# Pools of their own for k and v, weight buffers in the place of k, and four chunks of the first feed-forward product ahead of the second

## The chip, the cores and the metric

The kernel runs on one core of a Trainium2 chip. The time is the device time of one execution in microseconds (us); the median of three runs is 2384.47 us. TensorE (PE) multiplies, VectorE (DVE) and ScalarE (ACT) do the elementwise work, GpSimd (POOL) and SyncE (SP) here mostly start transfers (DMA). Each of them works off its own queue in order: an instruction that waits holds all that stand behind it.

## The reference

Two layers, each with a normalisation ahead of it and a residual around it, over x of 2 x 2048 x 1024 in float32 (4096 tokens, width C = 1024):

```python
x = x + attn(layernorm(x), Wqkv, bqkv, Wo, bo)       # one head of width D = 256
x = x + ffn(layernorm(x), gate_w, up_w, down_w, fc1_w, fc2_w, expert_w, ln_gamma, ln_beta)

def ffn(h):
    w = sum(top_2(h @ gate_w))                        # of 8 experts, per token
    shared = relu(h @ up_w) ** 2 @ down_w             # 1024 -> 2048 -> 1024
    routed = ((h @ fc1_w) @ expert_w * w) @ fc2_w     # 1024 -> 512 -> 512 -> 1024
    return layernorm(shared + routed) * ln_gamma + ln_beta
```

## The kernel before, in words

Every product is made of three matmuls: each operand is split into a high part (a cast to fp32r, by ACT) and a low part (the rest, a subtraction, by DVE), and high x high, low x high and high x low are added up in one PSUM bank (`Pass3`, L117). All matmuls of this kind have line L130; tile names tell them apart: ps scores, po values, pw projection behind attention, pu first feed-forward product, pd second one.

The tokens are worked in eight blocks of 512 (NBLK = 8); blocks 0 to 3 are the first batch, 4 to 7 the second.

1. Q, K and V of all blocks (`qkv_block`, L408). k and v of a block are "units", tiles of 8 KB in each partition. Those of blocks 4 to 7 go to DRAM and are read back when the second batch begins (L530, L726, L755).
2. Attention (L709 to L761): for n = 1 to 8 the scores of block n, 16 chunks k of keys, are made beside the values of block n-1. `softmax` (L578) of a pair of chunks is: DVE subtracts the maximum (L586), ACT takes the exponential (L587), ACT and DVE split the result into p (L142, L143), DVE adds up the sum (L593, L595). `values` (L597) then needs 12 matmuls for the pair. `finish` (L608) takes o out of PSUM (L614, L615) and sums over partitions (psum, L619), and `project` (L629) multiplies with Wo: it loads the residual row (L634, SP), adds the bias by a DMA of POOL (L635), and DVE adds each result to it (L646), which SP stores to x1 (L649). In round n = 8 no scores are left: PE has the values of block 7 and its projection only. In the same round the normalised x of block 0 is fetched in transposed form by SP (xt, L740) and split into X["p1"] and X["p2"], its two halves, four pieces each (`split_x`, L743).
3. Feed-forward (from L764), for pairs of blocks b = 0 to 3: both products are made by a Strassen-like scheme with seven products p1 to p7. A product has NK = 10 chunks, each with a weight piece w of 4 KB in a partition and 12 matmuls. The first product's order is `UP` (L772): p1 runs one chunk ahead of p2, which adds into p1's banks; then p4, p6, p5, p3, p7. `next_piece` (L829) keeps the pieces coming: `stage` (L786) loads one (SP, L798), `cast_piece` casts (ACT, L815), `end_piece` subtracts (DVE, L823) and stores some of the split pieces for later use (w_p, POOL, L826). Three pieces are ready, one is cast, two are staged. Beside the first chunks of b = 0 the second block of the pair is normalised (`norm2`, with rows loaded by SP through L192 at m = 0, 1, 2 and 4), the gate is computed (`gate_part`, L867), and from m = 13 X["p4"] is split for chunk m = 20.

Memory: the pool `ex` (6 units, 48 KB) holds k4, v4, k5, v5, k6 and v6 in the second batch; k7 and v7 lie in the pool `unit`. `ex` is closed at L764, and `wp` opens in its place: gamma (4 KB), seven weight buffers w (28 KB), four buffers sp (16 KB) for the second product. PSUM has eight banks: four in psa (po, pw, pu), two in psb (scores, every third pu), two in psc (small results).

What sets the order: the feed-forward part is written under a manual schedule, which keeps its written order on each engine. Attention is not: there a planner places instructions, by its own estimates of when each is ready, and it also places the feed-forward's first instructions among attention's last ones. What it places stays in that order on each queue, whatever the real times.

Of the kernel before, what the change touches and what calls it, by code (L numbers as in the profile page):

```python
# [9 lines left out]
FP = mybir.dt.float32  # L10
FR = mybir.dt.float32r
# [6 lines left out]
P = 128  # L18
SQ = 32
W = 512  # L20
U = 2048
# [4 lines left out]
def kernel(  # L26
# [21 lines left out]
    nc = tc.nc  # L48
    B, S, C = x.shape
# [10 lines left out]
    NB = W // P  # L60
    NBLK = NT // W
# [12 lines left out]
    psa = ctx.enter_context(tc.tile_pool(name="psa", bufs=4, space=PSUM))  # L74
    psb = ctx.enter_context(tc.tile_pool(name="psb", bufs=2, space=PSUM))
    psc = ctx.enter_context(tc.tile_pool(name="psc", bufs=2, space=PSUM))

    ex_guard = tc.tile_pool(name="ex", bufs=6)
    ex = ex_guard.__enter__()

    def unit(name, dtype=FR):
        return up.tile([P, U], dtype, tag="u", name=name)

    def ex_unit(name, dtype=FR):
        return ex.tile([P, U], dtype, tag="u", name=name)

    def row(name):
        return rp.tile([P, C], FP, tag="r", name=name)
# [4 lines left out]
    def bank(pool, name):  # L93
        return pool.tile([P, W], FP, tag="b", name=name)
# [147 lines left out]
    def split_x(xts, half, t, X, split=split):  # L242
        xv = xts[t].rearrange("p (a k j) -> p k a j", k=NCC, j=SQ)[:, ts(half, NCC // 2)]
        hi, lo = (
            v.rearrange("p (c n) -> p c n", n=W)[:, :, ts(t, P)].rearrange(
                "p c (a j) -> p c a j", j=SQ
            )
            for v in X
        )
        split(xv, hi, lo)  # L250
# [103 lines left out]
    NK = (NIC + NLC) // 2  # L354
# [102 lines left out]
    order = list(range(BPB, NBLK)) + list(range(BPB))  # L457
# [171 lines left out]
    def project(n):  # L629
        s = st.pop(n)  # L630
        o = hl(s["oT"])
        for t in range(NB):
            r = row("xres")
            nc.sync.dma_start(out=r, in_=xf[ds(n * W + t * P, P), :])  # L634
            last[0] = nc.gpsimd.dma_start(  # L635
                out=r, in_=bo.partition_broadcast(P), accum_op=ALU.add
            )
            for h in range(C // W):
                pm = bank(psa, "pw")
                acc = Pass3(pm, NDC)  # L640
                for dc in range(NDC):
                    acc.add(
                        tuple(o[:, i, ds(dc * W + t * P, P)] for i in range(2)),
                        piece(wo, dc, C, ts(h, W)),
                    )
                nc.vector.scalar_tensor_tensor(  # L646
                    r[:, ts(h, W)], pm, s["ri"][:, t : t + 1], r[:, ts(h, W)], ALU.mult, ALU.add
                )
            nc.sync.dma_start(out=x1[n][ts(t, P), :], in_=r)  # L649
# [38 lines left out]
    with tc.manual_schedule():  # L688
# [3 lines left out]
        for i in range(NBLK - 1):  # L692
            norm, xT, x3 = a_block(i, norm, xT, x3)
            if i == 0:
                for h in range(C // W):
                    nc.gpsimd.dma_start(
                        out=cols(fc2e, h, W), in_=fold[h].rearrange("p (c n) -> p c n", n=W)
# [10 lines left out]
    xts = []  # L708
    for n in range(1, NBLK + 1):  # L709
        if n == NBLK:  # L710
            X = {p: (unit("xh"), unit("xl")) for p in ("p1", "p2")}

        lag = LAG if n > 1 else LAG + 2
        for k in range(NKC + lag):
            if n + 1 < NBLK:
                if k == 0:
                    q_row = load_row(q_d[n + 1])
                elif k == NKC // 2:
                    start(n + 1, q_row)
            if n < NBLK and k < NKC:  # L720
                scores(n, k)
            if k >= lag:
                values(n - 1, k - lag)
                if n == BPB and (k - LAG) % 4 == 3:
                    j = BPB + (k - LAG) // 4
                    kv[j].append(load_kv(f"v{j}", v_d[j], kv_home(j)))  # L726
            if n == 1 and k == 1:
                softmax(0, 0)
            if n == 1 and k % 2 and 1 < k < NKC:
                softmax(0, k // 2)  # L730
            elif n > 1 and k % 2 == 0 and k + 2 < NKC:
                softmax(n - 1, k // 2 + 1)

            if k == NKC // 2 and n in range(2, 2 + NB):
                xts.append(load_row(x1[0][ts(n - 2, P), :]))
            elif k == 5 and n in range(3, 3 + NB):
                xts[n - 3] = norm_row(xts[n - 3], nc.sync)
            elif n == NBLK:
                if k < NB:
                    xts[k] = fetch_tile(xts[k], nc.sync)  # L740
                elif k % 2 == 0 and k >= 6 and k < 6 + 2 * NB:
                    for h, p in enumerate(X):
                        split_x(xts, h, k // 2 - 3, X[p])  # L743
            if k in (2, 8) and n > 1 and steps:
                with tc.issue_after(last[0].ins):
                    sum_step(steps.pop(0))
            if n == 1 and k == NKC // 2:
                wo = unit("wo_h"), unit("wo_l")
                for dc in range(NDC):
                    split(wo_f[dc], *(v[:, ts(dc, C)] for v in wo))  # L750
                split(g_f, gate[:, :, 0:NE], gate[:, :, NE : 2 * NE])
            if k == NKC - 1:
                if n == BPB - 1:
                    for j in range(BPB, 2 * BPB):
                        kv[j] = [load_kv(f"k{j}", k_d[j], kv_home(j))]  # L755
                if n < NBLK:
                    row_max(n)
        finish(n - 1)
        if n < NBLK:
            softmax(n, 0)  # L760
        project(n - 1)  # L761


    ex_guard.__exit__(None, None, None)  # L764
    wp = ctx.enter_context(tc.tile_pool(name="wp", bufs=1))
    gamma_sb = wp.tile([P, C], FP, name="gamma")
    nc.gpsimd.dma_start(out=gamma_sb, in_=ln_gamma.partition_broadcast(P))


    RIGHT = {"p1": (0, 0), "p2": (1, 0), "p3": (1, 1), "p4": 4, "p5": 1, "p6": 2, "p7": 3}  # L770

    UP = [("p1", 0)]  # L772
    for i in range(NK):
        UP += ([("p1", i + 1)] if i + 1 < NK else []) + [("p2", i)]
    UP += [(p, i) for p in ("p4", "p6", "p5", "p3", "p7") for i in range(NK)]
    DOWN = [(p, i) for p in ("p1", "p2", "p6", "p5", "p3", "p7", "p4") for i in range(NK)]
    NBB = NBLK // 2
    pieces = [(b, s, *w) for b in range(NBB) for s in range(2) for w in (UP, DOWN)[s]]
    kept, staged, cast, ready = {}, [], [], []
    LATE = 5  # L780

# [4 lines left out]
    def stage():  # L786


        b, s, p, i = pieces.pop(0)
        if len(pieces) < LATE and early:  # L790
            staged.append((early.pop(0), False, None))
            return
        w = wp.tile([P, 2 * W], FR, tag="w", name="w", bufs=7)
        if (s, p, i) in kept:
            nc.sync.dma_start(out=w.bitcast(FP), in_=kept[s, p, i])
            staged.append((w, False, None))
            return
        nc.sync.dma_start(out=as_piece(f32(w)[:, W : 2 * W], s), in_=source(s, RIGHT[p], i))  # L798

        staged.append((w, True, (s, p, i) if b == 1 or i % 2 == 0 else None))  # L800

    early = []

    def load_early(i):

# [202 lines left out]
    with tc.manual_schedule():  # L1008
        for b in range(NBB):
            if b == 0:  # L1010
                norm2 = Norm(1)
            x_t = [t1, None]

            h = {}
# [17 lines left out]
            sp_sum, sp_cast, sp = [], [], []  # L1032
# [15 lines left out]
            def cast_s(t=None):  # L1048
                v, a12 = sp_sum.pop(0)
                if t is None:  # L1050
                    t = wp.tile([P, 2 * W], FR, tag="sp", name="sp", bufs=4)
                nc.scalar.copy(t[:, 0:W], v)  # L1052
                sp_cast.append((v, t, a12))

# [19 lines left out]
            def next_s():  # L1074
                more_s(2)
                return sp.pop(0)

            rwb, acc = [None, None], {}
            n_bank[0] = 1
            for m, (p, i) in enumerate(UP):  # L1080
                flush()
                w = next_piece()
                if p != "p2":
# [44 lines left out]
                    out_step()  # L1128
                if b == 0 and m in (0, 1, 2, 4, 6, 8, 9, 10, 11, 12, 13):
                    norm2.step()  # L1130

                m4 = 12 if b == 0 else 10
                if m == m4:
# [4 lines left out]
                elif m >= 2 * NK and p != "p7":  # L1138
                    n = {"p4": "p6", "p6": "p5", "p5": "p3", "p3": "p7"}[p]
# [5 lines left out]
                        r_, f_ = PLACE[n]  # L1145
                        split_x(x_t[r_], f_, i // 2, X[n], split_late)

                if m == 0:
                    ga = half("ga")[: 2 * NE, :]
                    nc.scalar.copy(ga, gate_part(X["p1"], 0))  # L1150
                elif m == 2:
                    gs = half("gs")[: 2 * NE, :]
                    add(gs, ga, gate_part(X["p2"], 1), ALU.add)
                    gt = Gate(gs)
                elif (p, i) == ("p4", 1):
                    add(ga, ga, gate_part(X["p4"], 1), ALU.add)
                elif (p, i) == ("p7", 0):
                    add(ga, ga, gate_part(X["p7"], 0), ALU.subtract)
                    gt = Gate(ga)
# [6 lines left out]
            X = {}  # L1166
# [15 lines left out]
            for j, p in enumerate(("p1", "p2", "p6", "p5", "p3", "p7", "p4")):  # L1182
# [12 lines left out]
                for k in range(NK - late):  # L1195
                    flush()
                    w, s = next_piece(), next_s()
                    for t in range(NB):
                        down(t, s, w)
                    if more:  # L1200
# [3 lines left out]
                        if j >= 5 and k % 2 and k < 2 * NB:  # L1204
                            n = "p1" if j == 5 else "p2"
# [15 lines left out]
                if late:  # L1221
                    last_w = [next_piece() for _ in range(late)]
                    both = unit("last")
                    while len(sp) < late:
                        i = len(sp) + len(sp_cast) - late + 2
                        step_s(both[:, ts(i, 2 * W)] if sp_sum and i >= 0 else None)
                    last = [(sp.pop(0), w) for w in last_w]
                for t in range(NB):
                    for s, w in last if late else ():
                        down(t, s, w)  # L1230
                    ps, u, v = accs[t].ps, y_at(1, 0, t), y_at(1, 1, t)
# [72 lines left out]
```

## Time and profile before

| what | value |
|---|---|
| median of three runs | 2384.47 us (2383.08 to 2388.02) |
| profiled execution | 2384.76 us, span 2382.9 us |
| granted PE clock, mean | 0.995 |
| PE busy | 98% of the span |
| DVE, ACT, POOL busy | 61%, 47%, 13% |
| last scores of attention end | about 719.5 us |
| projection of the last block (pw) | 779.3 to 790.7 us |
| first chunk of p4 starts | 851.65 us |

Times in the profile are in us from the start of the span. In a timeline each line has start, length, engine, line of the code and tile, then the count, and in brackets how long the engine had been idle and who released it. In a list of waits, "A <- B: total, times, longest" says that A waited for B. PE's matmuls overlap, so its steps are read from one start to the next. SPq is the DMA queue of SP.

### The profile page before, as it was taken

What the parts mean: (1) busy time and instruction counts of PE and PEld (TensorE: products, weight loads), DVE (VectorE), ACT (ScalarE), POOL (GpSimd) and SP (SyncE); (2) the same over time, 40 slices, a digit from 0 to 9 for tenths busy, and PEclk for the clock granted to TensorE, in tenths of its full rate; (3) what the DMA queues carried; (4) which work ended last, traced back from release to release, by engine and by line L of the source; (5) the groups of instructions that cost most, each with busy time, mean ns of one, the idle gap of its engine ahead of it and who ended that gap; (6) DMA issues with size and microseconds to landing.
All of it is one profiled execution on the core that took longest, in us unless ns stands there. A gap on an engine that the chain in (4) does not pass through costs nothing.

```text
span 2382.9 us, 29281 instructions
## 1 busy us (share of the span) xinstructions
PE 2335.8 (98%) x10704; PEld 1921.8 (81%) x10704; DVE 1461.4 (61%) x2168; ACT 1131.4 (47%) x1846; POOL 298.1 (13%) x450
## 2 busy tenths in 40 slices
PE   8999999999998999999999999999999999999998
PEld 7888878888886778788778888878888877888886
DVE  5566459888877466697746467644446563445545
ACT  6555455555444543676552374644145454214224
POOL 3222111012110010011210011210000010000001
PEclk9999999999999999999999999999999999999999
DMA  5977884999996666787997789997557798655695
GB/s 196 318 257 269 278 204 127 298 315 319 290 239 181 219 228 185 228 271 259 336 309 241 237 283 333 319 342 241 193 194 262 264 330 283 208 192 184 202 312 191
DMA packets 225807, 603.99 MB, mean 253 GB/s; under 512 B 18768, under 2 KB 80720, under 8 KB 223616
## 3 DMA queue, kind: packets, MB, share of 16 engines
q1 hardware_dynamic: 152160, 334.02, 41.2%
q0 software_dynamic: 73504, 268.11, 36.8%
q8 instruction: 85, 1.39, 0.2%
q14 instruction: 58, 0.48, 0.1%
HBM read 448.96 MB, written 210.76 MB: 277 GB/s over the span
## 4 chain that ended last, share of the span: by engine, by line
PE 88%; issue 5%; DMA 4%; DVE 1%; ACT 1%; POOL 1%; SPq 0%; POOLq 0%; DVEq 0%; ACTq 0%
PE pu L130 29%; PE pd L130 26%; PE ps L130 7%; PE pq L130 7%; PE po L130 7%; PE pv L130 4%; PE pw L130 3%; DMA w<-wt 1%; PE pg L872 1%; PE pf L130 1%; DMA xt<-xt_d 1%; DMA w<-w_p 1%; PE psum L619 1%; DMA res<-in_L_ffn_ln_beta_dram 0%; DMA ew<-in_L_ffn_expert_w_dram 0%
## 5 line engine op out<-in xcount | busy, mean ns | idle before, releaser
L130 PE MATMUL pd<-w,sp 128*128 128x512 f32 x3336 | 762.5, 390 | 11.0 <-DVE sp L1057 5.6
L130 PEld LDWEIGHTS pd<-w,sp 128*128 128x128 f32 x3336 | 626.5, 188 | 145.8 <-DVE sp L1057 8.4
L130 PE MATMUL pu<-xh,w 128*128 128x512 f32 x2240 | 694.4, 391 | 7.2 <-ACT w L815 5.1
L130 PEld LDWEIGHTS pu<-xh,w 128*128 128x128 f32 x2240 | 419.6, 188 | 99.0 <-ACT w L815 6.1
L130 PE MATMUL pu<-xl,w 128*128 128x512 f32 x1120 | 436.2, 389 | 0.0
L130 PEld LDWEIGHTS pu<-xl,w 128*128 128x128 f32 x1120 | 210.4, 188 | 44.1 <-DVE xl L150 0.4
L1052 ACT CAST sp<-h 128x512 fp32r<-128x512 f32 x238 | 145.9, 618 | 193.1 <-PE pd L130 160.7
L1057 DVE TENSOR_TENSOR sp<-h,sp 128x512 fp32r<-128x512 f32 x238 | 162.4, 687 | 100.9 <-ACT sp L1052 100.6
L815 ACT CAST w<-w 128x512 fp32r<-128x512 f32 x210 | 128.3, 617 | 178.4 <-DMA w<-wt 144.7
L130 PE MATMUL po<-p,v 128*128 128x512 f32 x768 | 197.0, 395 | 2.6 <-ACT p L142 2.4
L823 DVE TENSOR_TENSOR w<-w 128x512 fp32r<-128x512 f32 x210 | 143.1, 686 | 91.3 <-ACT w L815 84.8
L130 PE MATMUL ps<-q,k 128*128 128x512 f32 x768 | 195.9, 393 | 1.8 <-DVE max L562 1.8
L130 PEld LDWEIGHTS ps<-q,k 128*128 128x128 f32 x768 | 142.4, 188 | 36.1 <-DVE max L562 6.8
L130 PEld LDWEIGHTS po<-p,v 128*128 128x128 f32 x768 | 144.1, 190 | 33.6 <-ACT p L142 3.2
L1002 ACT ACTIVATE h<-h 128x1024 f32<-128x1024 f32 x48 | 50.7, 1055 | 208.7 <-DVE h L1110 159.7
L826 POOL DMA_DIRECT2D w_p<-w x140 | 75.1, 537 | 583.1 <-DVE w L823 532.3
L150 DVE TENSOR_TENSOR xl<-xt,xh 128x512 fp32r<-128x512 f32 x104 | 71.6, 688 | 122.8 <-ACT xh L149 120.8
L557 ACT COPY s<-ps 128x512 f32<-128x512 f32 x128 | 74.8, 585 | 148.2 <-PE ps L130 147.7
L213 DVE STREAM_TRANSPOSE xblk<-xrow 128x1024 f32<-128x1024 f32 x60 | 121.1, 2019 | 9.6 <-ACT xrow L283 9.6
L562 DVE TENSOR_TENSOR max<-ps,max 128x512 f32<-128x512 f32 x120 | 82.3, 685 | 44.4 <-ACT s L557 44.1
L130 PE MATMUL pq<-xha,w_h 128*128 128x512 f32 x256 | 99.7, 389 | 0.0
L130 PE MATMUL pq<-xha,w_l 128*128 128x512 f32 x256 | 99.7, 389 | 0.0
(181 smaller groups left out, 3034.3 us busy)
## 6 DMA issues: line engine op xcount, KB each, us to landing
w<-w_p SPq DMA_DIRECT2D x350, 512.0 KB, 4.2
w_p<-w POOLq DMA_DIRECT2D x140, 512.0 KB, 4.8
w<-wt SPq DMA_DIRECT2D x210, 256.0 KB, 3.7
xt_d<-xblk POOLq DMA_DIRECT2D x56, 512.0 KB, 4.6
xt<-xt_d POOLq DMA_DIRECT2D x56, 512.0 KB, 6.6
wt<-in_L_ffn_up_w_dram POOLq DMA_DIRECT2D x9, 2048.0 KB, 25.1
wt<-in_L_ffn_down_w_dram POOLq DMA_DIRECT2D x9, 2048.0 KB, 32.3
xres<-in_L_attn_x_dram SPq DMA_DIRECT2D x32, 512.0 KB, 13.0
```

The source lines that it names most:

```text
L130: nc.tensor.matmul(self.ps, lhsT=a, rhs=b, start=self.i == 0, stop=self.i == self.n - 1, skip_group_check=self.on,)
L150: late_ops.append(lambda: nc.vector.tensor_tensor(lo, t, f32(hi), ALU.subtract))
L213: nc.vector.transpose(b.rearrange("p (q k i) -> p q k i", q=P // SQ, i=SQ), r.rearrange("p (k i q) -> p q k i", k=NCC, i=SQ),)
L557: nc.scalar.copy(s["s"][k // 4][:, ts(k % 4, W)], pm)
L562: nc.vector.tensor_tensor(s["max"], pm, s["max"], ALU.max)
L619: nc.tensor.matmul(pt[:, t : t + 1], lhsT=s["sum"][:, ds(i * W + t * P, P)], rhs=ones, start=i == 0, stop=i == 1,)
L815: nc.scalar.copy(w[:, 0:W], f32(w)[:, W : 2 * W])
L823: nc.vector.tensor_tensor(w[:, W : 2 * W], v[:, W : 2 * W], v[:, 0:W], ALU.subtract)
L826: nc.gpsimd.dma_start(out=kept[key], in_=w.bitcast(FP))
L1002: nc.scalar.activation(o, v, AF.Relu)
L1052: nc.scalar.copy(t[:, 0:W], v)
L1057: add(t[:, W : 2 * W], v, f32(t)[:, 0:W], ALU.subtract)
```

## The change

k and v get a pool each, of three units (`exv`, `exk`). When they close, four pools open in their place: gamma (4 KB), the four sp buffers (16 KB) and one weight buffer (4 KB) in the 24 KB where v was, six weight buffers (24 KB) in the place of k. Of each seven weight pieces the seventh takes the buffer in v's place. gamma's load moves to the head of the first product, b = 0.

For b = 0, p1 runs four chunks ahead of p2 instead of one; the gate's two products follow p1's chunk 4 and p2's chunk 0 (m = 4 and 5, where they were m = 0 and 2). In attention's last round only X["p1"] is split; X["p2"] is split beside the first four chunks. The projection of the last block takes its banks from psc instead of psa.

```diff
-    ex_guard = tc.tile_pool(name="ex", bufs=6)
-    ex = ex_guard.__enter__()
+    ex_guards = [tc.tile_pool(name=f"ex{a}", bufs=3) for a in "vk"]
+    ex = {a: g.__enter__() for a, g in zip("vk", ex_guards)}
...
     def ex_unit(name, dtype=FR):
-        return ex.tile([P, U], dtype, tag="u", name=name)
+        return ex[name[0]].tile([P, U], dtype, tag="u", name=name)
...
-                pm = bank(psa, "pw")
+                pm = bank(psa if n + 1 < NBLK else psc, "pw")
...
-                    for h, p in enumerate(X):
-                        split_x(xts, h, k // 2 - 3, X[p])
+                    split_x(xts, 0, k // 2 - 3, X["p1"])
...
-    ex_guard.__exit__(None, None, None)
-    wp = ctx.enter_context(tc.tile_pool(name="wp", bufs=1))
-    gamma_sb = wp.tile([P, C], FP, name="gamma")
-    nc.gpsimd.dma_start(out=gamma_sb, in_=ln_gamma.partition_broadcast(P))
+    for g in reversed(ex_guards):
+        g.__exit__(None, None, None)
+    gp = ctx.enter_context(tc.tile_pool(name="gp", bufs=1))
+    spp = ctx.enter_context(tc.tile_pool(name="spp", bufs=4))
+    wv = ctx.enter_context(tc.tile_pool(name="wv", bufs=1))
+    wk = ctx.enter_context(tc.tile_pool(name="wk", bufs=6))
+    gamma_sb = gp.tile([P, C], FP, name="gamma")
...
-    UP = [("p1", 0)]
-    for i in range(NK):
-        UP += ([("p1", i + 1)] if i + 1 < NK else []) + [("p2", i)]
-    UP += [(p, i) for p in ("p4", "p6", "p5", "p3", "p7") for i in range(NK)]
+    def up_order(lag):
+        order = [("p1", i) for i in range(lag)]
+        for i in range(NK):
+            order += ([("p1", i + lag)] if i + lag < NK else []) + [("p2", i)]
+        return order + [(p, i) for p in ("p4", "p6", "p5", "p3", "p7") for i in range(NK)]
+
+    UPS = [up_order(4 if b == 0 else 1) for b in range(NBLK // 2)]
...
-        w = wp.tile([P, 2 * W], FR, tag="w", name="w", bufs=7)
+        n_w[0] += 1
+        w = (wk if n_w[0] % 7 else wv).tile([P, 2 * W], FR, tag="w", name="w")
...
-                    t = wp.tile([P, 2 * W], FR, tag="sp", name="sp", bufs=4)
+                    t = spp.tile([P, 2 * W], FR, tag="sp", name="sp")
...
+            if b == 0:
+                nc.gpsimd.dma_start(out=gamma_sb, in_=ln_gamma.partition_broadcast(P))
...
-            for m, (p, i) in enumerate(UP):
+            for m, (p, i) in enumerate(UPS[b]):
...
+                if b == 0 and m < NB:
+                    split_x(x_t[0], 1, m, X["p2"], split_late)
...
-                if m == 0:
+                if (p, i) == ("p1", 0 if b else 4):
                     ga = half("ga")[: 2 * NE, :]
                     nc.scalar.copy(ga, gate_part(X["p1"], 0))
-                elif m == 2:
+                elif (p, i) == ("p2", 0):
```

More of the change, by code (lines that the diff above doesn't have):

```diff
@@ L761 @@
         project(n - 1)
-    ex_guard.__exit__(None, None, None)
-    wp = ctx.enter_context(tc.tile_pool(name="wp", bufs=1))
-    gamma_sb = wp.tile([P, C], FP, name="gamma")
-    nc.gpsimd.dma_start(out=gamma_sb, in_=ln_gamma.partition_broadcast(P))
-    RIGHT = {"p1": (0, 0), "p2": (1, 0), "p3": (1, 1), "p4": 4, "p5": 1, "p6": 2, "p7": 3}
-    UP = [("p1", 0)]
-    for i in range(NK):
-        UP += ([("p1", i + 1)] if i + 1 < NK else []) + [("p2", i)]
-    UP += [(p, i) for p in ("p4", "p6", "p5", "p3", "p7") for i in range(NK)]
+    for g in reversed(ex_guards):
[5 more added lines that the diff above has]
+    gamma_sb = gp.tile([P, C], FP, name="gamma")
+    RIGHT = {"p1": (0, 0), "p2": (1, 0), "p3": (1, 1), "p4": 4, "p5": 1, "p6": 2, "p7": 3}
+    def up_order(lag):
[4 more added lines that the diff above has]
+    UPS = [up_order(4 if b == 0 else 1) for b in range(NBLK // 2)]
     DOWN = [(p, i) for p in ("p1", "p2", "p6", "p5", "p3", "p7", "p4") for i in range(NK)]
     NBB = NBLK // 2
-    pieces = [(b, s, *w) for b in range(NBB) for s in range(2) for w in (UP, DOWN)[s]]
+    pieces = [(b, s, *w) for b in range(NBB) for s in range(2) for w in (UPS[b], DOWN)[s]]
     kept, staged, cast, ready = {}, [], [], []
@@ L800, in stage @@
         staged.append((w, True, (s, p, i) if b == 1 or i % 2 == 0 else None))
-    early = []
+    early, n_w = [], [0]
     def load_early(i):
```

## The prediction

> **What bounds the kernel now.** I read the busy times first, then the waits of TensorE (PE), then the one stretch where its waits lie together: the end of attention, 738 to 791 us.
>
> The page, part 1:
> ```profile
> PE 2335.8 (98%) x10704; PEld 1921.8 (81%) x10704; DVE 1461.4 (61%) x2168; ACT 1131.4 (47%) x1846; POOL 298.1 (13%) x450
> ```
> PE is the bound almost everywhere, so a change that leaves the matmuls alone can only win PE's idle time. The windows by stage (columns: busy us of PE, weight load, DVE, ACT, POOL with counts; granted clock; DMA share; GB/s) show where that is:
> ```profile
> 723.00:739.00 16.00, 16.00 (x80) 13.50 (x80) 14.89 (x18) 6.85 (x8) 0.00 (x0) 1.00 0.42 137
> 739.00:752.00 13.00, 13.00 (x59) 10.74 (x58) 11.70 (x13) 8.78 (x13) 0.87 (x2) 1.00 0.89 315
> 752.00:781.00 29.00, 19.04 (x67) 13.87 (x66) 15.72 (x19) 8.95 (x13) 4.75 (x7) 0.76 0.80 218
> 781.00:791.00 10.00, 10.00 (x46) 8.26 (x45) 5.52 (x8) 0.00 (x0) 0.00 (x0) 1.00 0.55 207
> ```
> One row stands out: 752 to 781, PE busy 19 of 29 us at a clock of 0.76. From 723 to 752 VectorE (DVE) is the full engine (26.6 of 29 us): it makes the softmax of the last block, and after the last scores PE has nothing but that block's values to do. PE's timeline there (start, length, what, idle before):
> ```profile
> 753.56 3.37 PE L130 MATMUL po<-p,v 128*128 128x512 f32 x12 [1.17 <-ACT p L142]
> 758.12 3.43 PE L130 MATMUL po<-p,v 128*128 128x512 f32 x12 [1.20 <-ACT p L142]
> 766.69 0.79 PE L130 MATMUL pu<-xh,w 128*128 128x512 f32 x1 [5.13 <-ACT w L815]
> 769.74 3.58 PE L619 MATMUL psum<-ones,sum 128*128 128x1 f32 x16 [2.26 <-DVE sum L595]
> ```
> The third line is the longest single wait: a first-product matmul (pu) stands in PE's queue ahead of the last values and waits for a weight cast. ScalarE (ACT) tells why:
> ```profile
> 757.02 1.04 ACT L142 CAST p<-s 128x1024 fp32r<-128x1024 f32 x1
> 766.02 0.62 ACT L815 CAST w<-w 128x512 fp32r<-128x512 f32 x1 [7.95 <-DMA w<-wt]
> 766.86 0.62 ACT L815 CAST w<-w 128x512 fp32r<-128x512 f32 x1 [0.22 <-DMA w<-wt]
> 767.38 1.05 ACT L587 ACTIVATE s<-s 128x1024 f32<-128x1024 f32 x1
> ```
> Two casts of weights stand ahead of the last exponential and hold it 7.95 us, though DVE had its input ready at 760.5. And the weights come late because of where their buffers lie; the SP queue's timeline and its waits:
> ```profile
> 741.05 4.20 SPq L634 DMA_DIRECT2D xres<-in_L_attn_x_dram  x4
> 756.96 7.41 SPq L798 DMA_DIRECT2D w<-wt  x5
> ```
> ```profile
> SPq L798 <- PE po L130: 11.7, 1, 11.7
> ```
> SP is free at 745.3 and waits until 756.96 for the values that still read the bytes under the first weights.
>
> What the stretch loses: from 738.63 to 790.54 PE does 96 po, 6 pu and 48 pw matmuls. The chain of waits has six full-speed ones in 1.36 us, so 150 x 0.2267 = 34.0 us, and the 16 psum matmuls of the block before took 1.68: 35.7 of 51.9 us. **16.2 us are lost here**, and no more than that is to be won here.
>
> **The change, part by part.**
>
> *Pools and weights.* The first six weight buffers lie in the place of k, last read by scores that end by 719.5. No operation is added. SP's program has nothing but a 29.9 us wait for a projection store between 684 and 731, so the five first loads can go at 712 to 731 or, behind those stores, from 741 to 745. Five loads took 7.41 us to issue: at the latest they are in by about 753, at the earliest before 725. The Trainium skill (DMA: Bandwidth & Descriptors, "Issuing engines are not separate DMA queues") speaks against that: all queues share the 16 DMA engines and interleave, so weights brought forward slow what is in flight, here the xt fetches (landing 745.5 to 748.9) that the same p1 chunks need. At 739 to 752 the share is 0.89: there five loads would cost up to 7.4 us; at 723 to 739 it is 0.42 and SP idle, and there nothing. I take nothing, with 7.4 us as the far end. The 7.95 us ACT hold goes with it. What is late next is DVE.
>
> *Half of the early splits.* Four L142 casts and four L143 subtractions (p2) leave the values: DVE loses 4 x 0.64 = 2.5 us before the last p. They come back at m = 0 to 3 in the first product, together with 4 or 5 weight subtractions of 0.62 us (1.86 for three), 2.5 to 3.1 us. The two cancel.
>
> *Four p1 chunks ahead.* 4 x 12 matmuls, 10.9 us of PE work that needs only X p1 (splits done about 752) and weights. No matmul is added; they move into idle time. The new end of the stretch, from DVE's rows: the last subtraction L586 ends 760.5; exp 1.06, hi 1.05, lo 1.22 bring 763.8; 12 values 2.7, and 0.5 to the first projection matmul: 767. From 752.4 to 767 PE has 14.6 us for 36 values (8.2) and psum (1.7), so 4.7 us of p1 fits; 6.2 us is left over, then 10.9 of pw: 767 + 17.1 = 784. From PE's side alone: 738.63 + 192 x 0.2267 + 1.68 = 783.8. Both agree. Before, the same work (pw and four chunks) would end at 790.54 + 42 x 0.2267 = 800.1. I allow 1.5 us for chunks that stand in PE's queue a little too early, so 785.5 and a **gain of 14.6 us**; 16.2 if none does.
>
> Of the 16.2 lost, some is clock, not waiting: psum took 3.58 instead of 1.68, and the eleven or so matmuls after it start 0.43 apart. The Trainium skill (TensorE: Matmul & The Clock Gate, "Part 1: The HAM clock gate") says the clock halves after an idle window of about 3.4 us and needs a busy one to return. By the rows alone the third gap costs its 5.1 us; by the rule it also costs some 4 us of slow matmuls after it. With p1 between the values no gap over 3.4 us is expected, so both go; should one such gap stay, the rule adds about 1.7 us.
>
> *pw in two banks of psc instead of four of psa.* DVE evicts in 0.75 us, PE fills a bank in 1.36, so the pair holds if DVE is free; now DVE idles 0.61 us ahead of each of these evictions. One 0.69 us operation in between delays PE by a few tenths: 0 to 2.4 us for eight halves, I take 0.7.
>
> *gamma* moves to the head of the first product's program, on POOL: ahead of the w_p stores, which then wait with it until the values release it (757). The first store left at 770.85 before. Nothing. *Gate* one chunk nearer to its use (p2 0 at m=5, used at m=6): 2.7 us of cover for a 0.68 us addition; nothing, 2 us at most.
>
> *After the projection.* Here lies the unknown cost. Row loads of the second normalisation stand on SP between the weights (m = 0, 1, 2, 4), and wait for rows that the last projection frees. Before, at the end of pw, weights for 5.5 chunks were in hand (15 us). After, four are used up: w4 and w5, 2 chunks of 2.72 and two gate products of 1.85 (the chain of waits), 9.1 us. The seventh load went at 789.16, 1.5 us ahead of that end, and weights take 4.5 us to land and 1.3 to split: ready 4.3 us after it. It holds with 5 us to spare, but later waits of SP lose cover:
> ```profile
> SPq L798 <- DMA w_p<-w: 20.8, 6, 8.9
> ```
> Now PE lost under 2 us to them (0.46, 0.29, 1.11 at 829 to 852). Bounds: -2 (these go) to +16 (20.8 less the 5 to spare). The near row is what these waits cost now: I take +1.5.
>
> *k and v loads of the second batch* (479 to 546) go to slots of their own kind, so earlier or at the same time; PE shows no wait there. Nothing. The rest of the program keeps its order and the same turn of seven buffers.
>
> Sum: 14.6 - 0.7 - 1.5 = 12.4 us. The profiled execution took 2384.76 us (span 2382.9), 0.3 over the median of 2384.47. 2384.5 - 12.4 = 2372.
>
> **The rivals.**
>
> *B, gain half returned.* p4 begins when the second block is normalised, transposed and fetched (851.65, 61 us after the projection). Its rows come free only in the projection, and now 16 chunks instead of 20 cover the chain. If it runs by its own latencies (DMA share was 0.91 at 828 to 852), p4 starts 61 us after the new end of pw: 784 + 61 = 845, a gain of 6.7: 2378. Against it: the steps are tied to m, so the chain moves with PE.
>
> *C, no change.* The weights are not free earlier (a pool's buffers are handed on only when both pools close), so the loads go at 757 again and the chunks fill little. Or the four chunks fill, but all comes back. For it: the planner misjudged this very place before (5.13 us). Against: the wait named is po, and k isn't read by po. 2384.
>
> *D, slower.* The weight ring runs dry behind the projection, at m = 6 to 20. SP's waits for w_p stores and rows are exposed: 16 us, and two gaps over a clock window add 3.4: 19.4 against 14.6, less 0.7 of pw: 5.5 us slower, 2390. It decides from about 14 us of exposed waiting. For it: cover falls from 15 to 9 us. Against: SP can issue a load every 1.5 us, PE uses one in 2.72, so cover grows back.
>
> **How the numbers follow.** The likeliest (A) 58%: 2368 to 2377. B 19%, 2377 to 2380. C 13%, D 10%. A measurement can tell about 0.2% (4.8 us) from no change: faster is below 2379.7. All of A and most of B are: 0.75; the rest of B and C give 0.14, slower 0.11. The range 2366 to 2384 takes in the full 16.2 with the small waits gone, and reaches into C.
>
> **What would show it.** Right: the SP wait of L798 for po is gone and the first weights leave before 745; ACT has no wait for w ahead of the last exp; pu matmuls lie between po ones from 752; the clock of that stretch is near 1; the last pw with four chunks done ends by 784 to 787. Wrong: a PE wait over 2 us for w or xh at 752 to 770 (order), for w at 790 to 830 (D), or for xh ahead of p4 (B).

## The result and the profile after

| | before | after |
|---|---|---|
| median | 2384.79 us (2382.54 to 2389.92, 6 runs) | 2368.53 us (2367.43 to 2372.63, 6 runs) |
| ratio | | 0.9938, 95% interval 0.9927 to 0.9948 |
| profiled execution | 2384.76 us, span 2382.9 | 2368.20 us, span 2366.3 |
| granted PE clock, mean | 0.995 | 0.998 |

The kernel became 16.3 us faster; 12.4 were forecast, and 2368.5 lies in the forecast range. In the windows that were shown of before (busy us of PE, weight load, DVE, ACT, POOL; clock; DMA share; GB/s), PE has nothing idle left:

```profile
739.00:752.00 13.00, 13.00 (x59) 10.74 (x59) 13.00 (x14) 8.25 (x11) 1.72 (x2) 1.00 1.00 350
752.00:781.00 29.00, 29.00 (x136) 23.80 (x135) 17.55 (x22) 7.93 (x12) 3.34 (x5) 1.00 0.87 251
```

29 of 29 us, where it was 19.04, and the clock is 1.00, where it was 0.76. PE's timeline shows how the values end (start, length, what):

```profile
754.24 0.39 PE L130 MATMUL pu<-xh,w 128*128 128x512 f32 x1
754.46 4.70 PE L130 MATMUL po<-p,v 128*128 128x512 f32 x20
759.00 0.39 PE L130 MATMUL pu<-xh,w 128*128 128x512 f32 x1
...
760.58 1.07 PE L130 MATMUL po<-p,v 128*128 128x512 f32 x4
761.49 1.84 PE L619 MATMUL psum<-ones,sum 128*128 128x1 f32 x16
```

No line has a wait in brackets, and psum takes 1.84 us instead of 3.58. ACT goes from the last exponential straight to its cast, with no weight in between:

```profile
757.94 1.06 ACT L587 ACTIVATE s<-s 128x1024 f32<-128x1024 f32 x1 [3.82 <-DVE s L586]
759.03 1.05 ACT L142 CAST p<-s 128x1024 fp32r<-128x1024 f32 x1
765.11 1.28 ACT L614 CAST o<-po 128x512 fp32r<-128x512 f32 x2 [5.03 <-PE po L130]
```

The first five weights leave at 709.37, 48 us sooner than before. What SP waits for now is the scores, not the values; the timeline of SP and its waits:

```profile
709.37 3.32 SPq L808 DMA_DIRECT2D w<-wt  x5
```
```profile
SPq L808 <- PE ps L130: 24.1, 1, 24.1
```

The stretch can be counted as in the prediction, from the first value matmul after the projection of block 6 to the last pw matmul, at 0.2267 us for each matmul and 1.68 us for psum. Before, 16.2 us of it were lost; after, 157 matmuls and psum (37.3 us) take 37.65: 0.4 are lost. So 15.8 us come from here. A further 2.1 come between the projection and p4 (starts of matmuls that come late by more than PE's pace add up to 3.9 us there before and to 1.8 after): from the point where pw and four chunks are done (800.1 before; 777.6 + 34 x 0.2267 = 785.3 after) to the first eviction of p4 it took 54.9 us (855.0) and takes 52.8 (838.1). Against that, the stretch begins 1.1 us later (739.73 instead of 738.63); 0.8 of these are there when the first scores start (309.2, 310.0), long before the change. That makes 16.8 us; 16.6 are left at the end of the span.

### The profile page after: what moved, and what is told of

Its sections match the earlier page's. It is cut to its first block, busy times and chain, and to the rows that moved or that the text cites. A ratio compares the mean times of both kernels' runs of the same rounds, so it can differ in the third digit from the quotient of the medians.

```text
span 2366.3 us, 29281 instructions
## 1 busy us (share of the span) xinstructions
PE 2329.5 (98%) x10704; PEld 1918.7 (81%) x10704; DVE 1461.0 (62%) x2168; ACT 1131.6 (48%) x1846; POOL 298.4 (13%) x450
## 4 chain that ended last, share of the span: by engine, by line
PE 90%; DMA 4%; issue 3%; DVE 2%; ACT 1%; POOL 0%; SPq 0%; POOLq 0%; DVEq 0%; ACTq 0%
PE pu L130 31%; PE pd L130 26%; PE po L130 7%; PE pq L130 7%; PE ps L130 7%; PE pw L130 4%; PE pv L130 4%; PE pg L882 1%; PE pf L130 1%; DMA w<-wt 1%; DMA w<-w_p 1%; DMA res<-in_L_ffn_ln_beta_dram 1%; DMA w_p<-w 1%; PE psum L619 1%; DVE w L833 0%
```

## The experiments

"Lost" is PE's lost time in the stretch, counted as above from each kernel's trace; "half clock" is how long the granted clock was 0.50 in the stretch. Slow clock outside the stretch is not in the column: three pools for k had 13.65 us of it at 702, the pools alone 3.4 us at 721.6, one chunk ahead 3.4 us at 788.5.

| kernel | median, us | ratio to before (95%) | lost, us | half clock, us |
|---|---|---|---|---|
| before | 2384.79 | | 16.2 | 13.65 |
| changed kernel | 2368.53 | 0.9938 (0.9927 to 0.9948) | 0.4 | 0 |
| the same again | 2369.80 | 0.9937 (0.9925 to 0.9950) | 0.4 | 0 |
| new pools alone | 2371.92 | 0.9950 (0.9938 to 0.9963) | 1.7 | 0 |
| new order alone | 2378.99 | 0.9979 (0.9973 to 0.9986) | 12.6 | 13.65 |
| six weights in the place of v | 2376.79 | 0.9975 (0.9964 to 0.9985) | 10.5 | 10.24 |
| X p2 split early | 2371.30 | 0.9946 (0.9934 to 0.9958) | 1.9 | 0 |
| projection in psa | 2369.18 | 0.9935 (0.9923 to 0.9947) | 0.3 | 0 |
| p1 one chunk ahead | 2373.98 | 0.9956 (0.9944 to 0.9969) | 0.9 | 0 |
| k4's place first | 2371.12 | 0.9945 (0.9931 to 0.9958) | 0.4 | 0 |
| three pools for k | 2381.05 | 0.9987 (0.9979 to 0.9996) | 0.4 | 0 |
| ring of six, shifted | 2394.42 | 1.0046 (1.0033 to 1.0058) | 11.6 | 10.24 |
| ring of six, in k | 2382.48 | 0.9995 (0.9985 to 1.0004) | 0.4 | 0 |
| first casts behind the scores | 2366.66 | 0.9930 (0.9915 to 0.9944) | 0.4 | 0 |

Two theories stood at the start: (1) the place of the weights is what counts; (2) the four chunks as filling are.

**The new pools alone.** The order, the splits and the banks are those of before, gamma's load stays at the head of the first product.

```diff
-                    split_x(xts, 0, k // 2 - 3, X["p1"])
+                    for h, p in enumerate(X):
+                        split_x(xts, h, k // 2 - 3, X[p])
...
-    UPS = [up_order(4 if b == 0 else 1) for b in range(NBLK // 2)]
+    UPS = [up_order(1) for b in range(NBLK // 2)]
...
-                pm = bank(psa if n + 1 < NBLK else psc, "pw")
+                pm = bank(psa, "pw")
...
```

> The new pools alone: order, splits of X and banks of the projection as before. Theory 1 (the place of the weights is what counts: it takes the ScalarE hold of 8 us, the long PE wait and the slow clock behind it away): PE needs few filling matmuls, p1's chunks 0 and 1 have 24 of them and only 14 were used, so most of the gain is here; the four early p2 subtractions cost up to 2.5 us on VectorE. 2369 to 2373 us, SP has no wait of L808's line for the values. Theory 2 (the four chunks as filling are what counts, the place only lets them start): less than half of the 16 us, 2377 or more.

Measured: 2371.92 us, 0.0050 of the 0.0062, as theory 1 has it. PE fills with 12 matmuls of p1 before the projection ends, and the stretch loses 1.7 us.

**The new order alone**, with the pools of before:

```diff
-    ex_guards = [tc.tile_pool(name=f"ex{a}", bufs=3) for a in "vk"]
+    ex_guards = [tc.tile_pool(name="ex", bufs=6)]
...
-        w = (wk if n_w[0] % 7 else wv).tile([P, 2 * W], FR, tag="w", name="w")
+        w = wp.tile([P, 2 * W], FR, tag="w", name="w", bufs=7)
```

> The new order, late p2 splits and the two banks, with the pools of before. Theory 1: the first weights still wait for the values until about 757, the casts still stand ahead of the last exponential; only the 2.5 us of p2 subtractions are saved and the clock stays low behind the gap: 2380 to 2384 us. Theory 2: four chunks fill PE once the weights are in, and half or more of the gain comes: 2370 to 2377 us.

Measured: 2378.99 us, between the two expectations: theory 1 was right on the mechanism, and the time lies 1 us under its range. The waits of SP and the timelines of PE and ACT in this kernel:

```profile
SPq L805 <- PE po L130: 9.9, 1, 9.9
```
```profile
768.36 0.80 PE L130 MATMUL pu<-xh,w 128*128 128x512 f32 x1 [7.75 <-ACT w L822]
768.95 3.41 PE L619 MATMUL psum<-ones,sum 128*128 128x1 f32 x16
```
```profile
759.63 1.06 ACT L587 ACTIVATE s<-s 128x1024 f32<-128x1024 f32 x1 [3.81 <-DVE s L586]
767.69 0.62 ACT L822 CAST w<-w 128x512 fp32r<-128x512 f32 x1 [7.00 <-DMA w<-wt]
768.21 1.04 ACT L142 CAST p<-s 128x1024 fp32r<-128x1024 f32 x1
```

The weight cast holds ACT for 7 us as before, now one step later: the exponential is through, and the cast of the last p waits. Of the 3.6 us that the order wins in the stretch (16.2 to 12.6), 2.4 are the two waits of 1.2 us among the values (84 of them now run without a gap), since DVE no longer subtracts for p2 there. Only 6 matmuls of the four chunks stand before the projection's end: without weights there is nothing to fill with.

**The place of v.** All of the change, but the pools change places, so that six weight buffers lie where v was.

```diff
-    ex_guards = [tc.tile_pool(name=f"ex{a}", bufs=3) for a in "vk"]
-    ex = {a: g.__enter__() for a, g in zip("vk", ex_guards)}
+    ex_guards = [tc.tile_pool(name=f"ex{a}", bufs=3) for a in "kv"]
+    ex = {a: g.__enter__() for a, g in zip("kv", ex_guards)}
```

> All of the change, but the two pools change places, so that six weight buffers lie where v was and one where k was. Nothing else differs. Theory 1: SP's first weight load waits for the values again (over 5 us, until about 757) and the time goes back to within 5 us of before: 2378 to 2384 us. Theory 2 (the order fills PE, wherever the weights lie): within 5 us of the changed kernel, 2368 to 2373 us.

Measured: 2376.79 us, 1.2 us under the range of theory 1 and outside that of theory 2. The wait for po is back, 10.0 us, and so are the hold of ACT and the long wait of PE:

```profile
762.88 0.62 ACT L825 CAST w<-w 128x512 fp32r<-128x512 f32 x1 [4.59 <-DMA w<-wt]
```
```profile
763.55 0.79 PE L130 MATMUL pu<-xh,w 128*128 128x512 f32 x1 [5.33 <-ACT w L825]
764.14 3.41 PE L619 MATMUL psum<-ones,sum 128*128 128x1 f32 x16
```

In the source this run changes nothing but the place, and it gives back some 9 of the 15 us. Six remain, near the 5 of the order alone. So the place is the cause of most of the gain. The rest of the change (order, late splits and banks together) is worth 5 to 6 us where the place is wrong, and 3 us where it is right (0.9950 to 0.9938).

**X p2 split early** in the changed kernel:

```diff
-                    split_x(xts, 0, k // 2 - 3, X["p1"])
+                    for h, p in enumerate(X):
+                        split_x(xts, h, k // 2 - 3, X[p])
...
-                if b == 0 and m < NB:
-                    split_x(x_t[0], 1, m, X["p2"], split_late)
```

> The changed kernel with both halves of X split in attention's last round, as before. If VectorE's chain sets the end of the values, four subtractions of 0.61 us put it off by 2.4 us, and PE, which has p1 chunks to fill with, still loses little: 2368.5 to 2371 us. If PE is full already (0.4 us lost in the stretch), nothing is lost: 2368.5. A rival by which the late splits are what counts: 2372 or more.

Measured: 2371.30 us. The intervals of this kernel and the changed one overlap, but the trace has the price: 1.9 us lost against 0.4, with one wait of PE among the values:

```profile
759.30 3.43 PE L130 MATMUL po<-p,v 128*128 128x512 f32 x12 [0.85 <-ACT p L142]
```

DVE ends the last p at 765.2 here, 23.7 us after the stretch began; in the changed kernel at 761.4, 21.7 us after. The four subtractions do lie on the chain, though PE has work to cover most of it.

**One chunk ahead**, with p2 split late (two pieces beside each of the first two chunks).

```diff
-    UPS = [up_order(4 if b == 0 else 1) for b in range(NBLK // 2)]
+    UPS = [up_order(1) for b in range(NBLK // 2)]
...
-                if b == 0 and m < NB:
-                    split_x(x_t[0], 1, m, X["p2"], split_late)
+                if b == 0 and m < NB // 2:
+                    for t in (2 * m, 2 * m + 1):
+                        split_x(x_t[0], 1, t, X["p2"], split_late)
...
```

> The changed kernel with p1 one chunk ahead of p2 as before; the p2 half of X is split beside the first two chunks (two pieces each) instead of the first four. If the lag of four is needed as filling, PE runs out of p1 work or waits for X p2 or the third and fourth weights beside the values: 2372 us or more. If the 14 matmuls that filled the stretch are all that counts, two chunks (24) do as well: within 2 us of the changed kernel.

Measured: 2373.98 us, 4.2 us over the changed kernel run beside it. That is the first side of the expectation (2372 or more), but not for want of filling: that is enough (12 matmuls, 0.9 us lost). The loss comes behind the projection: p2's first chunk stands there and its split isn't done.

```profile
787.32 0.73 PE L130 MATMUL pu<-xh,w 128*128 128x512 f32 x2 [1.71 <-ACT xh L149]
```

In this execution the clock is at 0.50 for 3.4 us behind that wait (10 matmuls in the time of 15), which adds some 1.7 us:

```profile
788.50:791.90 3.40, 3.40 (x10) 2.63 (x9) 0.18 (x1) 0.00 (x0) 0.00 (x0) 0.50 0.25 97
```

The four chunks are the cover of the p2 splits rather than the filling of the values.

**The projection in psa**:

```diff
-                pm = bank(psa if n + 1 < NBLK else psc, "pw")
+                pm = bank(psa, "pw")
```

> The changed kernel with the last projection in psa, as before. The banks of p1's chunks 1 and 2 lie in psa too and stay taken until p2, so the projection has two banks of psa at most, freed by the last values. If the two banks of psc cost nothing (no wait of the projection for an eviction was seen in the changed kernel) and psa gives two as well, the same within 1.5 us. If psc is needed because p1's early chunks hold psa, PE waits at the projection: 2 us slower or more.

Measured: 2369.18 us, the same. The two banks of psc cost nothing that can be measured, and psa would have done as well.

**A wait that moved.** In the changed kernel, the one run again, and the pools alone, PE has a gap among the last scores that before did not have: 0.3, 1.5 and 2.0 us at 717 to 720. ACT and then PE of the kernel with the pools alone:

```profile
718.49 0.62 ACT L826 CAST w<-w 128x512 fp32r<-128x512 f32 x1 [4.08 <-DMA w<-wt]
719.01 0.58 ACT L557 COPY s<-ps 128x512 f32<-128x512 f32 x1
```
```profile
720.37 1.91 PE L130 MATMUL ps<-q,k 128*128 128x512 f32 x6 [1.82 <-DVE max L562]
```

The casts of the first weights now stand among the evictions of the last scores, and wait for their loads there. It is the old hold, moved to where it costs 0.3 to 2 us. With the pools alone it costs more: behind this wait the clock is at 0.50 for 3.4 us, and PE does 9 matmuls in the time of 15.

```profile
721.60:725.00 3.40, 3.40 (x9) 2.52 (x8) 1.21 (x2) 0.59 (x1) 0.00 (x0) 0.50 0.00 0
```

Three tries at this wait follow.

*First, other buffers first*: the three pairs of weight buffers in the order k4, k5, k6.

```diff
-    wk = ctx.enter_context(tc.tile_pool(name="wk", bufs=6))
+    wks = [ctx.enter_context(tc.tile_pool(name=f"wk{i}", bufs=2)) for i in range(3)]
...
-        w = (wk if n_w[0] % 7 else wv).tile([P, 2 * W], FR, tag="w", name="w")
+        place = (n_w[0] - 1) % 7 // 2
+        w = (wv if place == 3 else wks[(1, 2, 0)[place]]).tile([P, 2 * W], FR, tag="w", name="w")
```

> The changed kernel with the first two weight buffers in the place of k4, the next two in that of k5 and the third pair in that of k6 (they began with k6). The instructions stand in the same order on every engine. In the changed kernel SP's first load waits for the scores of k6's keys until 709, and ScalarE's first casts of weights, which stand among the evictions of the last scores, wait 1.7 us (4.1 in the kernel with the pools alone) for these loads; PE then waits 0.3 to 1.8 us for a bank at 719. Theory: with k4 first the loads leave at 685 to 700, the hold and PE's wait go: 0.3 to 2 us faster than the changed kernel. Rival: the loads then meet the full DMA queues of 680 to 720 and land no sooner: same.

Measured: no gain (0.9945; 0.9937 for the changed kernel beside it), and the theory's first step is what failed: SP's wait is the same 24.1 us. It looks as if the buffers of a closed pool are handed on when the pool's last reader is done, whichever buffer is taken; the next run tests that.

```profile
SPq L809 <- PE ps L130: 24.1, 1, 24.1
```

*Second, a pool for each k*:

```diff
-    ex_guards = [tc.tile_pool(name=f"ex{a}", bufs=3) for a in "vk"]
+    ex_guards = [tc.tile_pool(name="exv", bufs=3)]
+    ex_guards += [tc.tile_pool(name=f"exk{i}", bufs=1) for i in range(3)]
...
-    wk = ctx.enter_context(tc.tile_pool(name="wk", bufs=6))
+    wks = [ctx.enter_context(tc.tile_pool(name=f"wk{i}", bufs=2)) for i in range(3)]
...
```

> The changed kernel with k in three pools of one unit, and a pool of two weight buffers in the place of each: first the one of k4, then k5, then k6. The kernel with only the order of buffers changed had the same wait of SP (24.1 us, until the scores of the pool's last k), so a pool seems to be handed on as a whole. Theory: with pools of their own the first two loads leave at 685 to 690 and the next at about 700; ScalarE's hold for weights among the last scores (1.7 to 5.6 us) and PE's wait at 719 (0.3 to 1.9 us) go: 0.5 to 2 us faster than the changed kernel. Rival: SP is not the limit, the DMA queues are full until 720 and the loads land when they did: same.

Measured: 2381.05 us, 12 us slower than the changed kernel, which neither theory had. The first loads left at 687.53, as meant, so a pool of its own is handed on by itself. But two casts now stood ahead of evictions of scores at 693 (presumably since the loads were ready sooner by the planner's estimate), and the loads did not land. SP, ACT and PE, then two windows:

```profile
687.53 36.12 SPq L815 DMA_DIRECT2D w<-wt  x5
```

```profile
708.92 0.62 ACT L832 CAST w<-w 128x512 fp32r<-128x512 f32 x1 [15.65 <-DMA w<-wt]
```
```profile
711.59 0.80 PE L136 MATMUL ps<-q,k 128*128 128x512 f32 x1 [13.67 <-DVE max L568]
```
```profile
690.00:702.00 12.00, 7.92 (x35) 6.21 (x34) 4.84 (x6) 3.27 (x4) 0.88 (x1) 1.00 1.06 298
702.00:715.60 13.60, 4.01 (x10) 3.18 (x11) 4.76 (x6) 4.77 (x8) 0.86 (x1) 0.50 0.55 126
```

A load issued at 687.53 that its cast sees at 708.9 took 21 us. For tile w in that part of the trace the times from issue to landing (min, median, max) are, in this kernel and then in the changed one:

```profile
DMA to landing us min/median/max: 2.8/13.8/21.7
```
```profile
DMA to landing us min/median/max: 3.2/6.7/6.9
```

In this kernel the DMA share is 1.06 from 690 to 702 and 0.55 from there; in the changed kernel it is 1.05 and, to 715, 0.59. So the engines are full when the early loads arrive, and have room by 709. The first load left 22 us sooner than in the changed kernel and landed only 3.7 us sooner (708.9 against 712.6): the rival had the landing right, but not what stands behind it. The rule weighed in the prediction (the Trainium skill, DMA: Bandwidth & Descriptors, "Issuing engines are not separate DMA queues": all queues share the 16 DMA engines) fits this, and the hold of 15.65 us is more than the 7.4 us that I gave it as the far end at a later time. PE stood still for over 13 us, and the clock was at 0.50 for the 13.6 us from 702.

*Third, the casts moved, not the loads*: the first ones are queued behind the last eviction of scores on ACT.

```diff
-        nc.scalar.copy(s["s"][k // 4][:, ts(k % 4, W)], pm)
+        last_s[0] = nc.scalar.copy(s["s"][k // 4][:, ts(k % 4, W)], pm)
...
         if raw:
-            nc.scalar.copy(w[:, 0:W], f32(w)[:, W : 2 * W])
+            n_cast[0] += 1
+            if n_cast[0] <= 5:
+                with tc.issue_after(last_s[0].ins):
+                    nc.scalar.copy(w[:, 0:W], f32(w)[:, W : 2 * W])
+            else:
+                nc.scalar.copy(w[:, 0:W], f32(w)[:, W : 2 * W])
```

> The changed kernel, with ScalarE's first weight casts put behind the last eviction of scores in its queue (they stood among the evictions); the loads and all else are as they were. Theory (a cast that waits for its load holds the evictions behind it, and PE with them): the hold of 1.7 to 5.6 us and PE's wait of 0.3 to 1.9 us at 719 go, and the weights are still ready by 728, 25 us before their first use: 0.3 to 2 us faster than the changed kernel, 0.9925 to 0.9937 of before. Rival: the casts now delay the first softmax of the last block by their 2.1 us, and VectorE's chain with it: same or up to 1 us slower.

Measured: 2366.66 us, 0.9930 of before. The gap is gone, as ACT and PE show; the whole is 0.0007 (1.7 us) under the changed kernel's 0.9937, though the intervals overlap.

```profile
721.12 0.59 ACT L559 COPY s<-ps 128x512 f32<-128x512 f32 x1 [2.13 <-PE ps L130]
721.61 2.18 ACT L830 CAST w<-w 128x512 fp32r<-128x512 f32 x4
726.32 1.06 ACT L589 ACTIVATE s<-s 128x1024 f32<-128x1024 f32 x1 [2.53 <-DVE s L588]
```
```profile
718.20 1.52 PE L130 MATMUL po<-p,v 128*128 128x512 f32 x6
719.56 1.52 PE L130 MATMUL ps<-q,k 128*128 128x512 f32 x6
```

The casts fall into time that ACT had free. It has the lowest median of all kernels here, by less than the noise.

**How near the ring of weights is to its edge.** First six buffers in turn by leaving out the seventh:

```diff
-        w = (wk if n_w[0] % 7 else wv).tile([P, 2 * W], FR, tag="w", name="w")
+        w = wk.tile([P, 2 * W], FR, tag="w", name="w")
```

> The changed kernel with six weight buffers in turn instead of seven, in all of the feed-forward part. Theory (the ring isn't near its edge, the cover behind the projection grows back): within 3 us. Rival (my prediction's slow case: SP's waits for the stores of weights are just covered by the ring): PE waits for weights in the first product and the time rises by 6 us or more.

Measured: 2394.42 us; but the run mixes two things. Without the seventh buffer the six slipped 4 KB down, the first into the place of v, SP waited 10.5 us for po, and the stretch lost 11.6 us. (So one buffer in the wrong place is enough.) The same with the place kept, by a gamma tile of twice the size:

```diff
-    gamma_sb = gp.tile([P, C], FP, name="gamma")
+    gamma_sb = gp.tile([P, 2 * C], FP, name="gamma")[:, 0:C]
...
-        w = (wk if n_w[0] % 7 else wv).tile([P, 2 * W], FR, tag="w", name="w")
+        w = wk.tile([P, 2 * W], FR, tag="w", name="w")
```

> The changed kernel with six weight buffers in turn, all in the place of k. (In the earlier kernel with six, the first one slipped 4 KB down into the place of v: SP's first load waited for the values again, and the stretch lost what it lost before.) What is left here is the price of a ring of six over the whole feed-forward part. Theory: the ring has little to spare, since 24 us could not come from the stretch alone: 5 to 12 us over the changed kernel. Rival: the ring has cover, all of the loss came from the place: within 3 us of the changed kernel.

Measured: 2382.48 us, 13.6 us over the changed kernel by the ratios, with 0.4 lost in the stretch: more than either side expected. It is the price of the seventh buffer over the whole feed-forward part. Most of it falls late: PE's starts that come late by more than its pace add up to 28.5 us behind the first pd matmul, against 17.1 in the changed kernel. Behind the projection, up to the first eviction of p4, they are 5.0 us against 1.8, of which 1.98 are one wait for X's split and the rest mostly 3.4 us at half clock behind it. Which wait of SP passes the loss on is not shown: its waits for stores of weights at L808 grow (61 times, 151.6 us; in the changed kernel 37 and 110.9), but those at the loads of kept pieces, L805, shrink by more (7 times, 26.8 us instead of 34 and 78.8). So the ring as a whole has almost nothing to spare, while at the place of the prediction's slow rival, behind the projection, even six buffers lose only some 3 us more.

## Why the prediction was right, point by point

1. *What is to be won.* 16.2 us lost, at most as much to win in the stretch: 15.8 were won.
2. *The weights.* Right: the wait for po went, the five loads left at 709.37 (the early end of the estimate was 712), the 7.95 us hold went, and the place alone is most of it. The choice to charge nothing for the shared DMA engines held for loads at 709, where the share falls to 0.59. It does not hold everywhere: the load of 687 took 21 us to land.
3. *"The two cancel."* This step failed. The p2 subtractions left DVE's chain, but the weight subtractions did not enter it: DVE made three of them at 713 to 719, among the scores. DVE after:

```profile
713.25 0.69 DVE L833 TENSOR_TENSOR w<-w 128x512 fp32r<-128x512 f32 x1 [2.56 <-ACT w L825]
717.02 0.69 DVE L833 TENSOR_TENSOR w<-w 128x512 fp32r<-128x512 f32 x1 [1.11 <-ACT w L825]
718.85 0.68 DVE L833 TENSOR_TENSOR w<-w 128x512 fp32r<-128x512 f32 x1
...
757.83 0.68 DVE L143 TENSOR_TENSOR xl<-xt,xh 128x512 fp32r<-128x512 f32 x1
759.03 1.23 DVE L595 TENSOR_TENSOR sum<-sum,s 128x1024 f32<-128x1024 f32 x1 [0.53 <-ACT s L587]
760.17 1.22 DVE L143 TENSOR_TENSOR p<-s,p 128x1024 fp32r<-128x1024 f32 x1
```

   The last p ended 21.7 us after the stretch began; by the prediction's numbers 25.2 (763.8 - 738.6). So the values needed less filling: 11 matmuls of p1 before the first one of the projection, where 4.7 us (21) had been fitted in. A second error stood beside this one: X p1 is not split by 752. Then only ACT's casts are done; DVE's last subtraction for it ends at 758.5 (the line at 757.83), and before, too, one of p1 and one of p2 stood at 760.43:

```profile
760.43 1.28 DVE L143 TENSOR_TENSOR xl<-xt,xh 128x512 fp32r<-128x512 f32 x2
```

   It did no harm, since PE had values to do: of p1 it did one matmul before 759.0. The 1.5 us that I had allowed for chunks standing too early were hardly needed (0.4 lost), so the stretch gave 15.8 us where I had put 14.6.
4. *The clock.* The rule that the prediction cites (the Trainium skill, TensorE: Matmul & The Clock Gate, "Part 1: The HAM clock gate": half the clock after an idle window of about 3.4 us) fits the fall of the clock before, but not the size. This is the window at the half clock:

```profile
764.70:778.30 13.60, 9.35 (x29) 7.78 (x30) 4.93 (x7) 4.17 (x6) 1.61 (x3) 0.50 0.68 226
```

   It begins 3.8 us after the values of 758.12 have run out (760.84), and lasts 13.65 us. Its 29 matmuls, 16 psum and 13 large ones, would take 1.68 + 13 x 0.2267 = 4.6 us; they were busy for 9.35. So 4.7 of the 16.2 us were slow clock. From the rows I had some 4; the 1.7 us that I took from the rule for one such gap are too few. In the stretch, all four kernels with a wait of over 5 us had 10 to 14 us at half clock, and no other had any. Outside it, a wait did not have to be that long: 1.82 us (the pools alone, 718.55), 1.71 us (one chunk ahead, 785.61) and 1.95 us (the changed kernel, 1138.16) each had 3.4 us at half clock begin within 1.3 us of their end, while behind 1.99 us at 279.5 in the changed kernel there was none. What decides is not shown.
5. *Two banks for pw.* 0.7 us charged, none found: psa gave the same time.
6. *After the projection.* +1.5 charged, -2.1 measured: the sign was wrong, and the value lies at the lower bound (-2). Of before's waits at 829 to 852 (0.46, 0.29, 1.11) one of 0.9 is left:

```profile
835.50 0.50 PE L130 MATMUL pu<-xl,w 128*128 128x512 f32 x1 [0.93 <-DVE xl L150]
```

   It stands in p4's first chunk and waits for the split of X p4, so the chain of the second block is only just in time. The loss of cover at this place was made good at once: the seventh load left 1.3 us before the end of pw (776.28), as estimated (1.5), and PE waited for no weight.
7. *What the prediction lacked.* The hold of ACT came back among the scores (0.3 to 2 us of PE). I had asked only whether the weights would be early enough, not what stands behind their casts.

Steps 3, 5 and 6 are 1.2 + 0.7 + 3.6 = 5.5 us better than forecast; the stretch began 1.1 us later, and 0.2 went behind p4: 4.2, the difference between 12.4 and the 16.6 us of the profile. The mechanism was right in its main part. The misses in the sum lie mostly on one side and don't cancel; that 2368.5 still lay in the range owes something to its width (2366 to 2384). Rival C fell with the two runs on the place. B did not show (the chain of the normalisation moved with PE: the first eviction of p4 came 16.9 us sooner), though the 0.9 us wait is of its kind. D did not start, and with six buffers the loss behind the projection was still small.

What stays open: the pools alone and the early p2 splits cost 2 to 3 us against the changed kernel, of which the stretch shows 1.3 and 1.5. With the pools alone the profiled execution adds the longer wait at 719 and some 1.7 us of slow clock behind it; the rest is within what single executions differ by. The moves of gamma and of the gate had no run of their own.

## What to carry to other kernels

Where a buffer lies is a dependency: the first load of a new stage waits for the last reader of what its pool took over, so give it the place that falls free first, and count who stands behind the first instruction that uses the load. Moving a load forward is not the same as having it sooner; a consumer that a planner then puts ahead of other work can cost more than the wait that was removed, and moving the consumer back can be better than moving the load forward. Where PE has a gap, look at the clock behind it: 4.7 of the 16.2 us lost here were slow matmuls, not waiting.

## What the runs showed that I had not expected

A closed pool's space is handed on as a whole: two orders of the buffers, and six of them instead of seven, gave the same 24.1 us wait of SP, and only separate pools changed it. In the kernel with three pools for k, a 256 KB load of weights took 2.8 us to land at best and 21.7 us where the DMA engines were full. One weight buffer of seven is worth 13.6 us (0.57%) in a kernel whose PE is busy 98% of the time. A wait of PE of 1.7 to 2 us can be followed by 3.4 us at half clock, which nearly doubles its price.
